# Tap stages with another order of evacuations and hooks, and gate chunks with one load beside the chunk at work

## The chip, the core and the metric

The kernel runs on one core of a Trainium2 chip. The metric is the device time of the program in microseconds (us); three runs of the kernel before gave a median of 1817.9 us (1817.29 to 1822.03). A profile is one further execution, which took 1812.46 us.

The engines are called as in the profile: PE is TensorE (PEld its weight loads), DVE is VectorE, ACT is ScalarE, POOL is GpSimd, SP is the engine that issues most transfers (DMAs). Each engine works through its own queue in order and waits on semaphores that others raise.

## What is computed

The input is x with shape (4, 256, 56, 56), all in float32. Four layers follow each other, each of the form x + f(gn(x)), where gn is a group norm over 32 groups of 8 channels.

```
layer 0, involution:  h = reduce_w . x;  kern = span_w . h + span_b   (7x7 taps for each of 16 groups and each pixel)
                      out[c, p] = sum over taps k of kern[group(c), k, p] * x[c, p + k]
layer 1:              two 3x3 convolutions with batch norms and relu, and a residual
layer 2, involution:  as layer 0, with a batch norm and relu after the reduction, a batch norm and relu at the end
layer 3, gates:       cf = mean over the image of real(fft2(xn)), per channel;  cf = sigmoid(cf @ W.T + b)
                      sf = real(fft2(mean over channels of xn)), per pixel
                      out = x + xn * cf + xn * sf,    xn = gn(x)
```

The mean of a two-dimensional Fourier transform is its input's first element, so cf needs only the pixel (0, 0) of every channel. sf is two small matrix products with cosines and sines of the 56x56 mean over the channels.

## The kernel before

`involution_layer` does layer 0 and, called a second time, layer 2; `conv_layer` lies between them and isn't touched. The loop of an involution runs over eight units, a unit being an image b (0 to 3) and a half cb of its channels (128 each). Each unit has two stages.

**Tap stage** (`tap_matrices`, L569). It makes the tap matrices kt of the unit in 32 steps, n = 0 to 31. In each step PE writes six matmuls (L580; the profile counts twelve[...]) into one PSUM tile of two banks. Then one engine moves the result with its bias to kt in SBUF: ACT in six instructions (L591) when n % 3 is 0, DVE in one (L598) otherwise. The pool `banks` has four such tiles, so PE can be at most four steps ahead of the evacuations. After step n the functions in `hooks[n]` are called: they put small pieces of other work at that place in each engine's queue. `place(hooks, g, (n1, n2, ...))` puts the generator g's successive pieces after steps n1, n2 and so on. A matmul of a hook takes a tile of the same pool.

**Column stage** (`apply`, L610). For each of seven columns tx, 8 pixels wide, PE multiplies the windows xw of the column with kt (L622), ACT and DVE gather the partial sums (`un`, L637 and L642), and in layer 2 DVE adds the result into the image block xs (L649). `next_windows` (L398) and `next_strip` (L362) prepare the column three further on: PE transposes a strip (L396), ACT copies it to xw (L408), and four transfers on SP's queue move it to the other row phases of xw (L414, L416). `late[tx]` holds functions that are called after column tx.

The hooks that the change touches lie in layer 2. Call (pb, pc) the unit before the one at work.

- `norm_of` (`norm_steps`, L200): six pieces, namely aggregate the statistics (DVE, L204), average over groups (PE, L207), copy and square the difference (DVE, L210 to L215), average again (PE, L218), add epsilon and take the power −1/2 (DVE L138, POOL L139), and make the shift (DVE, L222). It is placed at (2, 6, 7, 11, 12, 13) for the norm of layer 3. In the stages of units 1 and 2 of layer 2 a second norm is placed, that of layer 2's last image.
- `channel_mean` (L677) at (13, 17): small DVE work (L683, L694), then the mean over the channels on PE (L702, L705, two PSUM tiles), which is stored to DRAM.
- `gate_factors` (L720) when a whole image is done (pc is 1): loads the weights w3 (L725), multiplies them with the first pixels (PE, L732) and takes the sigmoid (ACT, L739), makes sf (PE, L748 and L762) and stores it to DRAM (L772).
- `load_step` (L963) loads the next image's block into the oldest of three blocks.

`gate_chunk` (L777) does layer 3's last line for images 0 to 2 on POOL, while the next image's units run. An image has 14 chunks: seven row bands j of 448 pixels times two halves cb. A chunk has two parts: the load of its piece of x from DRAM into one of three `gx` tiles, with the band's row of sf broadcast to all partitions (tile `sfb`, two buffers) when cb is 0; then four POOL operations (L789, L794, L795, L796) and the store (L797). `next_load` and `next_gate` start the next chunk's first and second part. POOL also issues these transfers. In the unit (b, 0) two loads stand after column 1 and a pair (gate, load) after each of columns 2 to 6; in (b, 1) three pairs stand in the tap stage (16, 22, 28) and six after columns 0 to 5. POOL's queue has little else in layer 2, so it works through the chunks as fast as transfers and the power of L139, which stands between them, let it.

At the end of a layer `in_order` ties every engine's instructions to the order in which the code wrote them. No scheduler moves them.

Of the kernel before, what the change touches and what calls it, by code (L numbers as in the profile page):

```python
# [10 lines left out]
F32 = mybir.dt.float32  # L11
AF = mybir.ActivationFunctionType
# [59 lines left out]
def net_kernel(  # L72
# [207 lines left out]
    def involution_layer(layer, xin, xout, red, span, sb, xs_of, ahead=None, pending=None):  # L280

        with ExitStack() as es:
# [23 lines left out]
            if layer == 0:  # L306
                load(0, 0, (2, 2, 2, 1))
                load(0, 1, (2, 2, 2, 1))

                nc.scalar.copy(norm_sb[:, 3, B - 1, 1, :], mhalf)  # L310

            red_sb = wpool.tile([P, NB, 2, R], F32, name="red_sb")

# [255 lines left out]
            def tap_matrices(b, cb, hooks):  # L569

                hp = h_of[b]
                kt = big.tile([Q, GB, TP // PB, NT, PB], F32, name="kt")
                for n in range(GB // 2 * TP // PB):
                    gp, pb = divmod(n, TP // PB)
                    ps = two_banks()
                    for k in range(PB):
                        py, px = divmod(pb * PB + k, TX)
                        z0 = ZF - py * QX - px
                        for i in range(2):
                            nc.tensor.matmul(  # L580
                                ps[:Q, i, k * NT : (k + 1) * NT],
                                z_sb[i * R : (i + 1) * R, cb * GB // 2 + gp, z0 : z0 + Q],
                                hp[i * R : (i + 1) * R, py, px].rearrange("p a t -> p (a t)"),
                                start=True,
                                stop=True,
                            )
                    g0, p0 = 2 * gp, pb * PB
                    if n % 3 == 0:
                        for i in range(2):
                            for k in range(PB):  # L590
                                nc.scalar.activation(  # L591
                                    kt[:, g0 + i, pb, :, k],
                                    ps[:Q, i, k * NT : (k + 1) * NT],
                                    AF.Identity,
                                    bias=zb_sb[:, cb * GB + g0 + i, p0 + k : p0 + k + 1],
                                )
                    else:
                        nc.vector.tensor_tensor(  # L598
                            kt[:, g0 : g0 + 2, pb],
                            ps[:Q, :, : PB * NT].rearrange("q i (k t) -> q i t k", k=PB),  # L600
                            zb_sb[:, cb * GB + g0 : cb * GB + g0 + 2, p0 : p0 + PB]
                            .unsqueeze(2)
                            .to_broadcast([Q, 2, NT, PB]),
                            ALU.add,
                        )
                    for h in hooks.get(n, ()):
                        h()
                return kt
# [68 lines left out]
            def channel_mean(b, cb):  # L677
# [39 lines left out]
                nc.sync.dma_start(m2_of[cb], m_dram[b][cb].rearrange("j (r w) -> (j r) w", w=W))  # L717
                yield

            def gate_factors(b):  # L720


                w3_sb = [dead(b, 1, 4 * CR * W + ci * C, C) for ci in range(NB)]
                for ci in range(NB):
                    nc.sync.dma_start(w3_sb[ci], w3[ci * P : (ci + 1) * P])  # L725
                cf = small.tile([P, NB], F32, name="cf")
# [36 lines left out]
                scale = small.tile([P, NB], F32, name="gscale")  # L763
                bias = small.tile([P, NB], F32, name="gbias")
                nc.vector.tensor_mul(scale, cf, norms[3][b][0])
                nc.vector.tensor_scalar_add(scale, scale, 1.0)
                nc.vector.tensor_mul(bias, cf, norms[3][b][1])
                gate_of[b] = scale, bias
                yield
                sf = small.tile([H, W], F32, name="sf", bufs=1)  # L770
                nc.vector.tensor_copy(sf, ps[:H, :W])
# [2 lines left out]

            sf_of, gate_of = {}, {}

            def gate_chunk(b, j, cb):  # L777

                rstd, shift = norms[3][b]
                at = slice(j * CR * W, (j + 1) * CR * W)  # L780
                if cb == 0:
                    sf_of[b] = work.tile([P, CR * W], F32, name="sfb", bufs=2)
                    nc.gpsimd.dma_start(sf_of[b], sf_dram[b][j : j + 1].to_broadcast([P, CR * W]))
                sf = sf_of[b]
# [4 lines left out]
                nc.gpsimd.tensor_scalar(  # L789
                    xn, xs, rstd[:, cb : cb + 1], shift[:, cb : cb + 1], ALU.mult, ALU.add  # L790
                )

                scale, bias = (t[:, cb : cb + 1] for t in gate_of[b])
                nc.gpsimd.tensor_scalar(xs, xs, scale, bias, ALU.mult, ALU.add)  # L794
                nc.gpsimd.tensor_tensor(xn, xn, sf, ALU.mult)  # L795
                nc.gpsimd.tensor_tensor(xs, xs, xn, ALU.add)  # L796
                nc.gpsimd.dma_start(ov[b, cb][:, at], xs)  # L797
                yield

# [193 lines left out]
            for u, (b, cb) in enumerate(units):  # L993
                hooks = hooks0 if u == 0 else {}
                if prev is not None:
# [726 lines left out]
```

## Time and profile before

| what | value |
|---|---|
| median of three runs | 1817.9 us |
| the profiled execution | 1812.46 us, its span 1810.7 us |
| mean granted clock of PE | 0.979 |
| PE busy | 1720.8 us, 95% of the span |
| DVE, ACT, POOL busy | 1375.4, 842.2, 430.0 us |
| layer 0's tap stages | 24.8 to 28.2 us each |
| layer 2, first tap stage to the last column stage's end | 1259.6 to 1778.4 us |
| of this, tap stages | 30.0, 31.8, 36.1, 29.1, 32.7, 28.7, 34.1, 31.0 us |
| of this, column stages | 28.3, 34.5, 31.5, 35.6, 34.4, 36.2, 32.3, 32.5 us |

How to read the profile: a row of a group or of a timeline has line, engine and operation, the tiles written and read, and in brackets how long the engine sat idle before it and what ended that. A stage is named here by the time at which it starts, counted from the start of the span. "Clock" is the share of its full clock that PE was granted; there are short periods at one half. A busy PE isn't necessarily at its peak. The chain of waits follows the work that ended last back from the end, at each step to what released it.

### The profile page before, as it was taken

How to read it: one execution, taken by the hardware profiler on the slowest of the kernel's cores; microseconds unless marked ns; L12 is line 12 of the kernel's file. 1: busy time of each engine (PE TensorE's matmuls, PEld its weight loads, DVE VectorE, ACT ScalarE, POOL GpSimd, SP SyncE). 2: the span in 40 equal slices, each digit the busy share in tenths (PEclk: the TensorE clock that was granted, in tenths of full speed). 3: DMA queues.
4: the chain of work that ended last, by engine and by line, in shares of the span. 5: the costliest groups of instructions: out<-in, count | busy, mean ns of one | idle time of the engine just before them, and what ended most of it. 6: DMA issues, size and time to landing. Idle time of an engine off the chain costs nothing.

```text
span 1810.7 us, 55835 instructions
## 1 busy us (share of the span) xinstructions
PE 1720.8 (95%) x24034; PEld 1514.9 (84%) x24034; DVE 1375.4 (76%) x2729; ACT 842.2 (47%) x1981; POOL 430.0 (24%) x626
## 2 busy tenths in 40 slices
PE   7999999999989999999999999997999999899988
PEld 6998989889878988998899889985988887887876
DVE  3787777776689988898889888875777677677775
ACT  3566556555532322322232222113767567577564
POOL 2333433245210000000000000000000374563572
PEclk9999999999989999999999999998999999999997
DMA  2545534454651201120121111031534566665653
GB/s 85 158 154 165 164 119 143 159 159 116 209 174 49 69 26 63 63 70 30 59 73 59 41 60 34 34 135 49 161 132 149 168 218 188 202 210 168 169 156 127
DMA packets 66004, 215.77 MB, mean 119 GB/s; under 512 B 13237, under 2 KB 20926, under 8 KB 62046
## 3 DMA queue, kind: packets, MB, share of 16 engines
q1 hardware_dynamic: 48718, 145.24, 25.7%
q0 software_dynamic: 14688, 64.78, 11.3%
q8 instruction: 190, 3.11, 0.7%
q10 hardware_dynamic: 2352, 2.18, 0.4%
q14 instruction: 56, 0.46, 0.1%
HBM read 76.30 MB, written 49.15 MB: 69 GB/s over the span
## 4 chain that ended last, share of the span: by engine, by line
PE 76%; DVE 9%; ACT 6%; DMA 4%; issue 2%; POOL 2%; SPq 1%; ACTq 0%; POOLq 0%; DVEq 0%
PE mm L1493 19%; PE ps L580 18%; PE ps L622 14%; PE mm L1411 10%; PE mm L1382 5%; PE ps L396 5%; DMA xw<-xw 4%; ACT kt L591 3%; PE ps L459 2%; DVE un L642 1%; DVE kt L598 1%; ACT xw L408 1%; ACT hp L478 1%; SPq L414 1%; DVE res L1486 1%
## 5 line engine op out<-in xcount | busy, mean ns | idle before, releaser
L580 PE MATMUL ps<-hp,z_sb 64*126 64x133 f32 x6144 | 392.1, 281 | 16.2 <-ACT kt L591 7.0
L622 PE MATMUL ps<-kt,xw 126*32 126x48 f32 (+1 forms) x12544 | 379.0, 236 | 24.1 <-DMA xw<-xw 12.1
L622 PEld LDWEIGHTS ps<-kt,xw 126*32 126x32 f32 (+1 forms) x12544 | 341.9, 122 | 68.2 <-issue 46.3
L580 PEld LDWEIGHTS ps<-hp,z_sb 64*126 64x126 f32 x6144 | 369.1, 187 | 34.6 <-ACT kt L591 12.7
L598 DVE TENSOR_TENSOR kt<-ps,zb_sb 126x798 f32<-126x798 f32 x336 | 319.8, 981 | 90.1 <-PE ps L580 89.5
L1493 PE MATMUL mm<-v,u_sb 128*128 128x280 f32 (+1 forms) x1728 | 385.0, 385 | 3.4 <-DVE v L1318 3.4
L1493 PEld LDWEIGHTS mm<-v,u_sb 128*128 128x128 f32 x1728 | 327.9, 190 | 57.5 <-DVE v L1318 3.8
L591 ACT ACTIVATE kt<-ps,zb_sb 126x133 f32<-126x133 f32 x1056 | 306.9, 442 | 96.2 <-PE ps L580 95.6
L1411 PE MATMUL mm<-v,u_sb 128*128 128x252 f32 (+1 forms) x936 | 212.3, 388 | 3.4 <-DVE v L1302 3.4
L1411 PEld LDWEIGHTS mm<-v,u_sb 128*128 128x128 f32 x936 | 178.3, 192 | 33.8 <-issue 3.5
L1530 POOL DMA_DIRECT2D x<-xs x24 | 13.1, 546 | 683.2 <-DVE xs L1529 427.4
L642 DVE SCALAR_TENSOR_TENSOR un<-ps,s,un 128x240 f32<-128x240 f32 x224 | 102.5, 457 | 85.7 <-ACT un L637 81.5
L642 DVE SCALAR_TENSOR_TENSOR un<-ps,par_sb,un 128x240 f32<-128x240 f32 x224 | 98.3, 457 | 87.1 <-ACT un L635 82.8
L1478 ACT ACTIVATE res<-xs,shift,norm_sb 128x1120 f32<-128x1120 f32 (+1 forms) x24 | 30.2, 1259 | 236.3 <-DVE xs L1529 107.3
L408 ACT COPY xw<-ps 126x896 f32<-126x896 f32 x112 | 101.4, 906 | 47.9 <-PE ps L396 37.7
L647 POOL TENSOR_TENSOR xs<-un,xs 128x240 f32<-128x240 f32 x112 | 72.3, 664 | 192.4 <-DVE un L642 192.3
L396 PE MATMUL ps<-ident_sb,strip_sb 128*126 128x128 f32 x784 | 111.7, 283 | 6.1 <-POOL strip_sb L381 5.8
L635 ACT ACTIVATE un<-ps,par_sb 128x240 f32<-128x240 f32 x112 | 50.1, 448 | 115.7 <-PE ps L622 113.4
L1382 PE MATMUL mm<-xs,u_sb 128*128 128x126 f32 (+1 forms) x792 | 98.6, 277 | 1.3 <-DVE xs L1345 0.9
L396 PEld LDWEIGHTS ps<-ident_sb,strip_sb 128*126 128x126 f32 x784 | 84.9, 142 | 17.0 <-POOL strip_sb L381 6.9
L637 ACT ACTIVATE un<-ps,bn_t,s 128x240 f32<-128x240 f32 x112 | 60.0, 538 | 83.3 <-PE ps L622 72.1
L1382 PEld LDWEIGHTS mm<-xs,u_sb 128*128 128x128 f32 x792 | 94.5, 191 | 2.4 <-issue 1.0
(254 smaller groups left out, 1925.8 us busy)
## 6 DMA issues: line engine op xcount, KB each, us to landing
xw<-xw SPq DMA_DIRECT2D x168, 252.0 KB
xw<-xw SPq DMA_DIRECT2D x224, 126.0 KB
xw<-xw POOLq DMA_DIRECT2D x56, 252.0 KB, 4.7
xs<-x SPq DMA_DIRECT2D x24, 560.0 KB
x<-xs POOLq DMA_DIRECT2D x8, 1568.0 KB, 8.2
xs<-x SPq DMA_DIRECT2D x8, 1568.0 KB
xs<-in_x_dram SPq DMA_DIRECT2D x6, 1568.0 KB
x<-xs SPq DMA_DIRECT2D x6, 1568.0 KB
```

The source lines that it names most:

```text
L396: nc.tensor.transpose(ps[:Q, k * P : (k + 1) * P], flat[:, k * Q : (k + 1) * Q], ident_sb)
L408: nc.scalar.copy(xw[:, :NSB, :], ps[:Q, : NSB * P].rearrange("q (n c) -> q n c", n=NSB))
L580: nc.tensor.matmul(ps[:Q, i, k * NT : (k + 1) * NT], z_sb[i * R : (i + 1) * R, cb * GB // 2 + gp, z0 : z0 + Q], hp[i * R : (i + 1) * R, py ...
L591: nc.scalar.activation(kt[:, g0 + i, pb, :, k], ps[:Q, i, k * NT : (k + 1) * NT], AF.Identity, bias=zb_sb[:, cb * GB + g0 + i, p0 + k : p0 ...
L598: nc.vector.tensor_tensor(kt[:, g0 : g0 + 2, pb], ps[:Q, :, : PB * NT].rearrange("q i (k t) -> q i t k", k=PB), zb_sb[:, cb * GB + g0 : cb ...
L622: nc.tensor.matmul(v[m * j : m * j + m, i, :, k * TP : (k + 1) * TP], xw[:, window(ty), m * j : m * j + m], kt[:, ng * j : ng * j + ng, :, ...
L637: nc.scalar.activation(part, o[0], AF.Identity, bias=bn["t4"][:, cb : cb + 1], scale=bn["s4"][ng][:, 0, cb : cb + 1])
L642: nc.vector.scalar_tensor_tensor(part, o[e], s, part, ALU.mult, ALU.add)
L647: nc.gpsimd.tensor_tensor(dst, u, dst, ALU.add)
L1382: nc.tensor.matmul(ps[:, co * m : (co + 1) * m], u[ci][:, co * P : (co + 1) * P], v2[:, e, : n // 2, ci * WT : (ci + 1) * WT], start=(ci = ...
L1411: nc.tensor.matmul(ps, u1_sb[:, ci, dy, k, co * P : (co + 1) * P], v[:, k, dy * NB + ci : (dy + n - 1) * NB + ci + 1 : NB, :], start=(j == 0),
L1493: nc.tensor.matmul(ps, u2_sb[:, ci, dy, k, co * P : (co + 1) * P], v[:, k, dy * NB + ci : (dy + n - 1) * NB + ci + 1 : NB, :], start=(j == 0),
```

## The change

Six things are changed, all in `involution_layer`.

- ACT's first instruction is a Sigmoid, in place of a copy. What it writes is overwritten later.
- ACT takes the steps with n % 3 equal to 2, not 0 (both involutions). So ACT has 10 steps in a stage and DVE 22, where it was 11 and 21.
- The second norm in units 1 and 2 of layer 2 moves to (15, 19, 20, 24, 25, 26).
- `gate_factors` begins at hook 8 with its load of w3, which goes into the two `sfb` buffers, and no longer into a dead part of the image block (the last image excepted).
- The gate is written as out = (sf + (cf + 1/rstd)) * xn − shift/rstd. It needs three POOL operations with one tensor operand and one with two, where it was two and two.
- The chunks: one load at hook 20 of the unit (b, 0), two bands of sf after column 0, then pairs (load, gate) after columns 1 to 5; four pairs in the tap stage of (b, 1) at 14, 18, 22, 26; five after its columns 0 to 4. The load of a chunk now stands in front of the chunk before it, so it writes the `gx` tile that was stored two chunks ago. The sf of band j + 2 is loaded at the end of band j.

```
-                nc.scalar.copy(norm_sb[:, 3, B - 1, 1, :], mhalf)
+                nc.scalar.activation(norm_sb[:, 3, B - 1, 1, :], mhalf, AF.Sigmoid)
...
-                    if n % 3 == 0:
+                    if n % 3 == 2:
...
+            def new_sf():
+                return work.tile([P, CR * W], F32, name="sfb", bufs=2)
...
-                w3_sb = [dead(b, 1, 4 * CR * W + ci * C, C) for ci in range(NB)]
+                w3_sb = [new_sf()[:, :C] if b < B - 1 else dead(b, 1, 4 * CR * W + ci * C, C) for ci in range(NB)]
...
-                nc.vector.tensor_mul(scale, cf, norms[3][b][0])
-                nc.vector.tensor_scalar_add(scale, scale, 1.0)
-                nc.vector.tensor_mul(bias, cf, norms[3][b][1])
-                gate_of[b] = scale, bias
+                nc.vector.reciprocal(back, rstd)
+                nc.vector.tensor_add(cfx, cf, back)
+                nc.vector.scalar_tensor_tensor(back, shift, -1.0, back, ALU.mult, ALU.mult)
+                gate_of[b] = cfx, back
...
+            def load_sf(b, j):
+                sf_of[b, j] = new_sf()
+                nc.gpsimd.dma_start(sf_of[b, j], sf_dram[b][j : j + 1].to_broadcast([P, CR * W]))
...
-                if cb == 0:
-                    sf_of[b] = work.tile([P, CR * W], F32, name="sfb", bufs=2)
-                    nc.gpsimd.dma_start(sf_of[b], sf_dram[b][j : j + 1].to_broadcast([P, CR * W]))
...
-                nc.gpsimd.tensor_scalar(xs, xs, scale, bias, ALU.mult, ALU.add)
-                nc.gpsimd.tensor_tensor(xn, xn, sf, ALU.mult)
-                nc.gpsimd.tensor_tensor(xs, xs, xn, ALU.add)
+                nc.gpsimd.tensor_scalar(xs, sf_of[b, j], 1.0, cfx, ALU.mult, ALU.add)
+                nc.gpsimd.tensor_tensor(xs, xs, xn, ALU.mult)
+                nc.gpsimd.tensor_scalar(xs, xs, 1.0, back, ALU.mult, ALU.add)
+                if cb == 1 and j + 2 < NCHUNK:
+                    load_sf(b, j + 2)
...
-                        place(hooks, g, (19, 20, 22, 23, 25, 26))
+                        place(hooks, g, (15, 19, 20, 24, 25, 26))
...
-                            place(hooks, gate_factors(pb), (17, 24, 27, 28, 30, 31))
+                            place(hooks, gate_factors(pb), (8, 24, 27, 28, 30, 31))
+                            chunks.extend(gate_chunk(pb, j, c) for j in range(NCHUNK) for c in range(NB))
+                            for n in (20,):
+                                hooks.setdefault(n, []).append(next_load)
...
-                        for n in (16, 22, 28):
-                            hooks.setdefault(n, []).extend((next_gate, next_load))
+                        for n in (14, 18, 22, 26):
+                            hooks.setdefault(n, []).extend((next_load, next_gate))
...
-                        chunks.extend(gate_chunk(b - 1, j, c) for j in range(NCHUNK) for c in range(NB))
-                        late[1] += [next_load, next_load]
-                    for tx in range(2, NTX) if cb == 0 else range(NTX - 1):
-                        late[tx] += [next_gate, next_load]
+                        late[0] += [lambda b=b, j=j: load_sf(b - 1, j) for j in range(2)]
+                    for tx in range(1, 6) if cb == 0 else range(NTX - 2):
+                        late[tx] += [next_load, next_gate]
```

More of the change, by code (lines that the diff above doesn't have):

```diff
@@ L762, in gate_factors @@
                 nc.tensor.matmul(ps[:H, :W], half, cs2_sb, start=True, stop=True)
-                scale = small.tile([P, NB], F32, name="gscale")
-                bias = small.tile([P, NB], F32, name="gbias")
-                nc.vector.tensor_mul(scale, cf, norms[3][b][0])
-                nc.vector.tensor_scalar_add(scale, scale, 1.0)
-                nc.vector.tensor_mul(bias, cf, norms[3][b][1])
-                gate_of[b] = scale, bias
+                cfx = small.tile([P, NB], F32, name="gscale")
+                back = small.tile([P, NB], F32, name="gbias")
+                rstd, shift = norms[3][b]
+                nc.vector.reciprocal(back, rstd)
+                nc.vector.tensor_add(cfx, cf, back)
+                nc.vector.scalar_tensor_tensor(back, shift, -1.0, back, ALU.mult, ALU.mult)
+                gate_of[b] = cfx, back
                 yield
@@ L780, in gate_chunk @@
                 at = slice(j * CR * W, (j + 1) * CR * W)
-                if cb == 0:
-                    sf_of[b] = work.tile([P, CR * W], F32, name="sfb", bufs=2)
-                    nc.gpsimd.dma_start(sf_of[b], sf_dram[b][j : j + 1].to_broadcast([P, CR * W]))
-                sf = sf_of[b]
                 xs = gx_tile()
@@ L791, in gate_chunk @@
                 )
[L793 to L796, printed above, removed]
+                cfx, back = (t[:, cb : cb + 1] for t in gate_of[b])
+                nc.gpsimd.tensor_scalar(xs, sf_of[b, j], 1.0, cfx, ALU.mult, ALU.add)
[3 more added lines that the diff above has]
+                    load_sf(b, j + 2)
                 nc.gpsimd.dma_start(ov[b, cb][:, at], xs)
```

## The prediction

> **What bounds the kernel now.** I read the page first, then a table of windows, one row for each tap and column stage, then the chain of waits inside layer 2, then the engines' timelines around each wait found there. The page names the bound:
>
> ```profile
> PE 1720.8 (95%) x24034; PEld 1514.9 (84%) x24034; DVE 1375.4 (76%) x2729; ACT 842.2 (47%) x1981; POOL 430.0 (24%) x626
> ```
>
> TensorE is the only full engine, so a stage can only gain what TensorE waits in it. The windows show where (after the length: busy us and instructions of PE, PEld, DVE, ACT, POOL, then clock, DMA share, GB/s):
>
> ```profile
> 159.30:184.10 24.80, 24.64 (x396) 23.87 (x395) 21.92 (x32) 19.83 (x67) 3.88 (x6) 1.00 0.46 163
> 1384.20:1420.30 36.10, 32.11 (x441) 28.35 (x440) 25.23 (x50) 23.50 (x73) 1.10 (x2) 0.95 0.36 127
> 1451.80:1480.90 29.10, 26.80 (x419) 24.28 (x418) 23.88 (x36) 21.58 (x70) 23.00 (x30) 1.00 0.72 240
> 1516.50:1549.20 32.70, 30.39 (x436) 26.46 (x435) 25.69 (x44) 22.45 (x72) 4.10 (x5) 1.00 0.43 153
> 1549.20:1583.60 34.40, 30.63 (x827) 27.52 (x826) 21.20 (x48) 18.18 (x26) 24.86 (x32) 0.90 0.74 205
> ```
>
> A layer-0 tap stage (first row) takes 24.8 us with almost no wait: 32 steps of about 0.75 us. Layer 2's last seven take 31.8, 36.1, 29.1, 32.7, 28.7, 34.1 and 31.0 us. Their hooks add at most 4.4 us of matmuls (channel mean 2.0, gate factors 1.8, second norm 0.6); the rest is wait or a lowered clock. Column stages without gates take 28.3 us (1289.6) or 34.5 (with the bottleneck); with gates 31.5 to 36.2. The chain inside layer 2 names what is waited for (start us, us, what):
>
> ```profile
> 1406.56 0.99 DVE kt L598
> 1409.63 1.75 ACT kt L591 x6
> ...
> 1539.02 2.30 DMA xs<-in_w_dram
> ...
> 1561.10 8.11 DMA xw<-xw
> ```
>
> And the engines' timelines give the single waits:
>
> ```profile
> 1404.57 0.30 PEld L207 LDWEIGHTS ps<-mv,gavg_sb 128*128 128x128 f32 x2 [1.11 <-ACT kt L591]
> 1408.31 0.30 PEld L218 LDWEIGHTS ps<-d,gavg_sb 128*128 128x128 f32 x2 [1.31 <-ACT kt L591]
> 1411.42 1.39 PEld L580 LDWEIGHTS ps<-hp,z_sb 64*126 64x126 f32 x12 [0.95 <-ACT kt L591]
> 1468.15 0.16 PEld L702 LDWEIGHTS ps<-one,mean 128*32 128x32 f32 x8 [1.25 <-DVE kt L598]
> 1411.39 1.28 ACT L739 ACT_TABLE_LOAD   x1
> 1465.63 1.57 DVE L694 TENSOR_SCALAR mean<-cmean,norm_sb 128x32 f32<-128x32 f32 x2
> 1517.46 1.07 DVE L649 SCALAR_TENSOR_TENSOR xs<-un,xs 128x240 f32<-128x240 f32 x1
> ```
>
> GpSimd is at 24% but not harmless: its groups in layer 2 (mean ns after the busy time) are
>
> ```profile
> L795 POOL TENSOR_TENSOR gn<-gn,sfb 128x448 f32<-128x448 f32 x42 | 49.0, 1166 | 0.0
> L796 POOL TENSOR_TENSOR gx<-gx,gn 128x448 f32<-128x448 f32 x42 | 48.7, 1160 | 3.3
> L794 POOL TENSOR_SCALAR gx<-gx,gscale,gbias 128x448 f32<-128x448 f32 x42 | 31.7, 756 | 4.2
> L789 POOL TENSOR_SCALAR gn<-gx,norm_sb 128x448 f32<-128x448 f32 x42 | 31.7, 754 | 24.4 <-DMA gx<-x 18.1 <-DVE un L642 5.3
> ```
>
> In DVE's timeline L649 takes 0.41 us when no GpSimd arithmetic runs, 0.86 on average (13 cases) under a GpSimd tensor_tensor; L694 takes 0.23 alone and 0.89 under one.
>
> [...] in the new program one table load is left. [...] a gx load lands 4.0 us after issue at 1551.8, and 8.6 us after at 1566.9, among xw transfers.
>
> **The change part by part.** Each sum is TensorE wait.
>
> *Sigmoid at the start, and w3 loaded at hook 8.* The first Sigmoid costs about 0.26 us (L739's rows) for a copy of 0.19, while ACT then idles 2.58 us for a DMA: nothing. The table load at 1411.39 goes. At hook 24 of the stage at 1384.2, step 25 waited 0.95 for ACT's step 24 (now VectorE's, done sooner) and step 26 0.19 for the Sigmoid: −1.1. At 1516.5 the w3 matmuls waited for their transfer, issued 1538.6 (0.69 + 0.49 of idle weight loads: −1.1), at 1648.6 2.0 us (the answer names ACT, which ended just then; w3's last packets run to 1672.5): −2.0. Now w3 is issued right behind the store of xs, some 16 us earlier, and its buffers' last gate is long over. **−4.2.** On SP nothing waits behind it; the next block's load, which waited for w3's readers (issued 1542.2 in the stage at 1516.5), can go at about 1538.5, and at both times lands before the column stage's xw transfers.
>
> *Second norm of layer 2's units 1 and 2 (stages 1318.0, 1384.2).* The statistics were aggregated at hook 19 and multiplied at hook 20, then used at 22 and multiplied at 23. One step (0.75 us) isn't enough: L204 ends at 1404.45 and L207 starts at 1404.57; the square ends 1408.2 and L218 starts 1408.31. Waits of 1.11 + 1.31 in each of two stages. The new places 15→19 and 20→24 leave four steps. Two tiles out of four PSUM buffers still cost about 0.2 each: **−4.0.**
>
> *ACT takes steps 2, 5, ... 29 (10 of them) instead of 0, 3, ... 30 (11).* In 16 stages one step moves from 6 × 0.29 us on ACT to 0.98 on VectorE. Three places count. (a) Hook 17: before, the channel mean's big tile took over step 15's buffer, an ACT step of 1.75 us, and its first matmuls queued behind VectorE's step 14. Now 15 is VectorE's, and 14 ACT's, so VectorE has 0.98 us more between the hook-13 work and step 15. Waits there: 0.32 in four stages, and 1.25, about 1.0 and 1.1 in the three (1451.8, 1583.6, 1714.9) where a gate chunk ran under L694. The new chunk issues a load (0.54) first and begins with two tensor_scalars, so L694 meets no tensor_tensor. Of 4.6 us: **−3.5**. (b) Start: VectorE now does 0, 1, [L1078], [L204], 3, 4 in a row, 0.98 + 0.95 + 0.54 + 0.33 + 0.95 + 0.9 = 4.65 us from 1386.09, so step 7 starts 0.4 us later than now; but ACT's strip no longer holds step 4 (wait 0.83), and L218 at hook 11, behind a wait for ACT of 0.25, comes at the same 9.8 us into the stage: 0, in layer 0 as well. (c) End: steps 30 and 31 are both VectorE's. At 182.63 it starts the first and ends the second at 184.55, where ACT ended step 30 at 184.38. Columns begin at 184.1 and need both: **+2.7** in 16 stages. The second norm in layer 0's stages (96.5, 213.2, 332.5) falls on worse places: step lengths now 1.09 + 0.92 + 1.09, 0.85 over; I work out 1.0: **+0.5.** The three new small operations at hook 30 have rows at 0.14 to 0.16 us in the last gates, like those that they replace.
>
> *Chunks: one load beside the chunk at work, three tensor_scalars and one tensor_tensor.* Arithmetic goes from 0.75 + 0.76 + 1.17 + 1.16 to 3 × 0.75 + 1.16, −0.43 us; with issues (0.54, 0.59, half of 0.55) and the 0.6 of gaps 5.6 becomes 5.2. The wait for a buffer's store (6.4 us in all) goes. GpSimd is off the path; what shows is when it runs. With 5 + 4 + 5 chunks for 5 + 3 + 6 the last should end before the next tap stage. Today it runs 3.4 us into it and slows L649 (1.07 and 0.85 us at 1517 to 1520): −1.0 there, −1.0 at 1714.9. **−2.0**; less tensor_tensor under the columns, **−0.5.**
>
> *DMA in the column stages.* The xw waits (1.1 at 1433, 3.8 at 1565, 2.1 at 1695) come at columns 3 to 5. Bytes are the same, and one of three first loads moves to hook 20. But two sfb loads go out at once, and the first store comes about 2 us sooner. Between 1558 and 1569, 2.3 MB moved in 11 us (208 GB/s): two transfers (0.46 MB) more in front of the xw cost 2.2 us, two fewer gain as much. I take **+1.0** over all.
>
> Sum: −4.2 − 4.0 − 3.5 + 2.7 + 0.5 − 2.0 − 0.5 + 1.0 = −10.0 us. The profiled execution took 1812.46 us (span 1810.7): 1802.5 for it. The timed runs' median is 1817.9, 5.4 us above; the same −10 gives 1808.
>
> **Rivals.** *The xw transfers lose (slower).* Place: columns 3 to 5 of six column stages with gates. For: DMA share is already 0.74, and above 0.9 at the wait. Price 2.2 us per two more transfers ahead, three give 3.3 × 6 = 20: 1808 + 20 = 1828. It decides from 2.6 us per stage on, where it beats the gain by 5.5. Against: the loads depend on one buffer each, so GpSimd slows itself when transfers are late. *The phase costs more (no change).* If VectorE's crowded start, of which I cost nothing, loses 0.4 us (step 7's delay) in all 16 stages, 6.4, and hook 17 gains half, the sum is −10 + 6.4 + 1.8 = −2: 1816. For: VectorE has 22 steps × 0.95 = 21 us of a 24.8 us stage. Against: its work catches up by hook 11. *The xw waits go (faster).* 7.0 at the three places above and about 2.5 at 1758 to 1768 in the last stage; with the +1.0 not spent, that is −20: 1798. For: one load fewer at the start, and the block's load earlier. Against: xw alone fills half of the DMA time.
>
> **How the numbers follow.** Forecast 0.50, xw waits go 0.16, no change 0.20, slower 0.14. A measurement tells 0.3% (5.5 us) from no change. The first two are faster: 0.66; same 0.20; slower 0.14. The range leaves out half of the two outer cases: 1800 to 1821; the likeliest case's own is 1802 to 1812, from half to one and a half of the sum.
>
> **What will show it.** Right: no table load at L739; no wait at L735 and L207/L218 above 0.3 us; the tap stages that now take 36.1, 32.7 and 34.1 come 2 to 4 us shorter; GpSimd idle at each tap stage's start in units after gates. Wrong if column stages with gates grow by over 2 us each, or layer 0's tap stages (24.8 and 26.2) by over 0.5. A throttle that falls on other stages (clock 0.90 at 1549.2 here) would move single stages without meaning.

## The result, and the profile after

| | before | after |
|---|---|---|
| median of five timed runs | 1820.47 us | 1800.78 us |
| their spread | 1817.29 to 1826.22 | 1798.91 to 1807.65 |
| the profiled execution, its span | 1812.46, 1810.7 us | 1803.55, 1801.8 us |

The ratio is 0.9907, with a 95% interval of 0.9882 to 0.9931: about 17 us less (12.6 to 21.5). A second measurement of the same kernel, told below, gave 0.9897 (0.9865 to 0.993). The forecast was 10 us less, so the sign is right and the size too small. The two profiled executions differ by only 8.9 us, and the experiments show why two single executions can't settle the size.

The page of the kernel after has one line for the engines:

```profile
PE 1717.5 (95%) x24034; PEld 1511.1 (84%) x24034; DVE 1389.1 (77%) x2745; ACT 815.6 (45%) x1884; POOL 403.8 (22%) x626
```

TensorE has the same 24034 matmuls and still sets the pace. ACT is busy 27 us less and VectorE 14 us more, GpSimd 26 us less. The table of windows for the same five stages as in the prediction (layer 0's stage, three tap stages, the column stage after the third; after the length, busy us and instructions of PE, PEld, DVE, ACT and POOL, then clock, DMA share and GB/s):

```profile
159.30:184.10 24.80, 24.65 (x417) 23.88 (x408) 22.62 (x34) 18.21 (x61) 3.89 (x6) 1.00 0.47 166
1384.90:1416.00 31.10, 30.07 (x441) 26.68 (x440) 25.89 (x51) 20.80 (x66) 1.65 (x3) 1.00 0.46 156
1451.60:1478.70 27.10, 26.66 (x419) 24.39 (x419) 23.70 (x37) 20.55 (x64) 14.10 (x21) 1.00 0.60 200
1513.90:1544.00 30.10, 29.32 (x437) 26.01 (x436) 24.97 (x44) 20.69 (x66) 2.15 (x4) 1.00 0.49 168
1544.00:1578.80 34.80, 29.44 (x829) 25.83 (x828) 20.54 (x48) 18.17 (x26) 22.91 (x33) 1.00 0.74 197
```

The tap stages of 36.1, 29.1 and 32.7 us became 31.1, 27.1 and 30.1. TensorE's idle time in them fell from 4.0, 2.3 and 2.3 us to 1.0, 0.4 and 0.8, and the clock of the first rose from 0.95 to 1.00. The column stage did not gain (34.4 to 34.8): its clock rose from 0.90 to 1.00, but TensorE idled 5.4 us in it where it had idled 3.8. In the timelines of the kernel after, the places of the second norm (L207, L218) and of the gates' weights w3 (now L735), and the one table load that is left (at the start, L310, where the kernel before has one too), read:

```profile
1403.05 0.30 PEld L207 LDWEIGHTS ps<-mv,gavg_sb 128*128 128x128 f32 x2
1407.05 0.30 PEld L218 LDWEIGHTS ps<-d,gavg_sb 128*128 128x128 f32 x2
1408.22 0.52 PEld L735 LDWEIGHTS ps<-first,sfb 128*128 128x128 f32 x4 [0.42 <-ACT kt L591]
1535.60 0.97 PEld L735 LDWEIGHTS ps<-first,sfb 128*128 128x128 f32 x8
```
```profile
L310 ACT ACT_TABLE_LOAD x1 | 1.3, 1283 | 2.9 <-issue 2.9
```

The brackets of 1.11 and 1.31 us at L207 and L218 are gone, and w3 is waited for in no stage. One wait of 0.42 us for an ACT step stays at L735. GpSimd's groups in layer 2 now have one tensor_tensor in place of two:

```profile
L799 POOL TENSOR_TENSOR gx<-gx,gn 128x448 f32<-128x448 f32 x42 | 48.4, 1153 | 3.5
L793 POOL TENSOR_SCALAR gn<-gx,norm_sb 128x448 f32<-128x448 f32 x42 | 31.3, 745 | 10.7 <-DMA gx<-x 9.4
L800 POOL TENSOR_SCALAR gx<-gx,gbias 128x448 f32<-128x448 f32 x42 | 27.6, 658 | 4.3
L798 POOL TENSOR_SCALAR gx<-sfb,gscale 128x448 f32<-128x448 f32 x42 | 27.5, 655 | 10.3 <-DMA sfb<-sf 6.5
```

The two tensor_scalars with one constant factor take 0.66 us, not the 0.75 that the prediction used, so a chunk's arithmetic fell by 0.6 us and not 0.43.

### The profile page after: what moved, and what is told of

Same layout as the page of the kernel before. It is cut to its first block, busy times and chain, and to the rows that moved or that the text cites. A ratio compares the mean times of both kernels' runs of the same rounds, so it can differ in the third digit from the quotient of the medians.

```text
span 1801.8 us, 55766 instructions
## 1 busy us (share of the span) xinstructions
PE 1717.5 (95%) x24034; PEld 1511.1 (84%) x24034; DVE 1389.1 (77%) x2745; ACT 815.6 (45%) x1884; POOL 403.8 (22%) x626
## 3 DMA queue, kind: packets, MB, share of 16 engines
q1 hardware_dynamic: 48718, 145.24, 25.9%
## 4 chain that ended last, share of the span: by engine, by line
PE 72%; DVE 16%; ACT 4%; DMA 3%; issue 3%; POOL 2%; SPq 1%; ACTq 0%; POOLq 0%; DVEq 0%
PE mm L1501 19%; PE ps L580 14%; PE ps L622 13%; PE mm L1419 10%; DVE kt L598 5%; PE mm L1390 5%; PE ps L396 3%; DVE un L642 3%; DMA xw<-xw 3%; PE ps L459 2%; DVE st L1086 1%; ACT kt L591 1%; ACT hp L478 1%; DVE res L1494 1%; PE ps L705 1%
## 5 line engine op out<-in xcount | busy, mean ns | idle before, releaser
L622 PE MATMUL ps<-kt,xw 126*32 126x48 f32 (+1 forms) x12544 | 380.1, 235 | 31.4 <-issue 18.0
L622 PEld LDWEIGHTS ps<-kt,xw 126*32 126x32 f32 (+1 forms) x12544 | 340.9, 121 | 77.5 <-issue 50.2
L580 PE MATMUL ps<-hp,z_sb 64*126 64x133 f32 x6144 | 383.5, 279 | 12.3 <-DVE kt L598 4.7
L580 PEld LDWEIGHTS ps<-hp,z_sb 64*126 64x126 f32 x6144 | 363.6, 185 | 28.3 <-DVE kt L598 6.4
L598 DVE TENSOR_TENSOR kt<-ps,zb_sb 126x798 f32<-126x798 f32 x352 | 333.1, 980 | 59.5 <-PE ps L580 59.1
L591 ACT ACTIVATE kt<-ps,zb_sb 126x133 f32<-126x133 f32 x960 | 280.1, 442 | 107.9 <-PE ps L580 107.8
L1419 PEld LDWEIGHTS mm<-v,u_sb 128*128 128x128 f32 x936 | 177.5, 191 | 31.8 <-issue 1.4
L1538 POOL DMA_DIRECT2D x<-xs x24 | 13.1, 546 | 682.3 <-DVE xs L1537 427.5
L396 PEld LDWEIGHTS ps<-ident_sb,strip_sb 128*126 128x126 f32 x784 | 84.6, 141 | 18.6 <-POOL strip_sb L381 6.6
L139 POOL TENSOR_TENSOR norm_sb<-norm_sb,mhalf 128x1 f32<-128x1 f32 x32 | 19.7, 619 | 350.1 <-DVE norm_sb L138 350.0
```

The source lines that it names most:

```text
L396: nc.tensor.transpose(ps[:Q, k * P : (k + 1) * P], flat[:, k * Q : (k + 1) * Q], ident_sb)
L580: nc.tensor.matmul(ps[:Q, i, k * NT : (k + 1) * NT], z_sb[i * R : (i + 1) * R, cb * GB // 2 + gp, z0 : z0 + Q], hp[i * R : (i + 1) * R, py ...
L591: nc.scalar.activation(kt[:, g0 + i, pb, :, k], ps[:Q, i, k * NT : (k + 1) * NT], AF.Identity, bias=zb_sb[:, cb * GB + g0 + i, p0 + k : p0 ...
L598: nc.vector.tensor_tensor(kt[:, g0 : g0 + 2, pb], ps[:Q, :, : PB * NT].rearrange("q i (k t) -> q i t k", k=PB), zb_sb[:, cb * GB + g0 : cb ...
L622: nc.tensor.matmul(v[m * j : m * j + m, i, :, k * TP : (k + 1) * TP], xw[:, window(ty), m * j : m * j + m], kt[:, ng * j : ng * j + ng, :, ...
L1419: nc.tensor.matmul(ps, u1_sb[:, ci, dy, k, co * P : (co + 1) * P], v[:, k, dy * NB + ci : (dy + n - 1) * NB + ci + 1 : NB, :], start=(j == 0),
```

## The experiments

Microseconds are the ratio times the median of before on that chip, with the interval in brackets. Three chips were used: one for the kernel before again, ACT's steps, the hooks and the first run of the chunks; a second for the gate's form, the places, the one-row stores and the later chunks; a third for the second norm, the kernel without the chunks, and the repeats of the chunks and of the kernel after. In code, line numbers move by up to 8 with each edit.

### The kernel before, measured against itself

No edit.

> The kernel before once more, for how much one execution differs from another. Theory A (each stage repeats itself, but for the throttle): layer 2's tap stages add up to 253.5 us again within 3 us, and the seven column stages before the last to 232.8 within 3 us plus half of what half-clock periods fall on them; the ratio of times is 1.000. Theory B (the waits for xw differ from execution to execution): the column stages with gates differ by 5 us or more in the sum, and the profile's 1810.7 us span was a lucky one; the next is 1815 or more.

Measured: 0.9998, −0.4 us [−4.4, +3.5]. The instructive part is its profile: the span was 1820.7 us against 1810.7 of the first, and layer 2's column stages took 275.8 us against 265.4, while its tap stages took 250.9 against 253.4. Column stages of one and the same kernel differ by 10 us from one execution to the next. So the 7.3 us by which they seem longer in the first profile of the kernel after (272.7) are no effect of the change. The tap stages repeat within about 3 us in all, so traces are compared there.

### ACT's steps alone

```
-                    if n % 3 == 0:
+                    if n % 3 == 2:
```

> Only the choice of ACT's steps (n % 3 equal to 2). By the forecast: hook 17 -3.5 (0.3 in four stages, 0.6 to 1.0 in the three under a gate chunk), stage ends +2.7, layer 0's second norm +0.5: together -0.3 us, ratio 1.000; the wait of step 3 or 4 at the stages' start goes and comes back at step 6. Rival (VectorE's crowded start costs 0.4 us per stage): +6, ratio 1.003.

Measured: 0.9996, −0.7 us [−4.4, +2.9]. The rival by which VectorE's crowded start would cost some 6 us is out. But the −3.5 us which the prediction booked at hook 17 aren't this edit's alone. In the timelines of this kernel, stage at 1459.5 (weight loads, then VectorE):

```profile
1474.50 0.19 PEld L702 LDWEIGHTS ps<-one,mean 128*32 128x32 f32 x8 [1.06 <-issue]
1475.33 0.16 PEld L705 LDWEIGHTS ps<-xs,mean 128*32 128x32 f32 x8 [0.64 <-DVE kt L598]
```
```profile
1472.68 1.71 DVE L694 TENSOR_SCALAR mean<-cmean,norm_sb 128x32 f32<-128x32 f32 x2
```

L694's pair still takes 1.71 us, and the channel mean is waited for twice, 1.06 and 0.64 us, where the kernel before had one wait of 1.25. In the four stages without a chunk at this place the matmuls' wait at L705 (0.24 us each) is gone, as forecast; in the three with one the wait is longer. What delays hook 17 in those is the GpSimd chunk, not ACT's step 15.

### The hooks alone, and the second norm alone

The Sigmoid at the start, w3 in the sf buffers at hook 8, and the second norm's places:

```
-                        place(hooks, g, (19, 20, 22, 23, 25, 26))
+                        place(hooks, g, (15, 19, 20, 24, 25, 26))
...
-                            place(hooks, gate_factors(pb), (17, 24, 27, 28, 30, 31))
+                            place(hooks, gate_factors(pb), (8, 24, 27, 28, 30, 31))
```

> Only the Sigmoid at the start, w3 at hook 8 in the sfb buffers, and the second norm's new places; ACT's steps and the chunks as before. By the forecast -4.2 - 4.0 = -8.2 us, ratio 0.9955, the stages that take 36.1, 32.7, 34.1 and 31.8 us shorter by 3.1, 1.1, 2.0 and 2.0. Rival (the gain in the tap stages is the phase's and the chunks'): -4 us or less.

Then only the first of the two pairs of lines:

> Of the hooks, only the second norm of layer 2's units 1 and 2 is moved; the table load, the w3 load and the gates' hooks stay as before. Forecast in the prediction: -4.0 us (waits of 1.11 and 1.31 us in each of two stages, less 0.2 for each tile). The traces' step lengths gave -5.2. So ratio 0.997 to 0.998. If instead the hooks' gain lies almost all in the gates' waits, -1 us or less (0.9995).

Measured: the hooks 0.9942, −10.5 us [−14.0, −7.1]; the second norm alone 0.9975, −4.5 us [−7.1, −2.2]. The forecasts were −8.2 and −4.0. The difference of the two, 6.0 us for the gates' hooks (from two chips), was forecast as 4.2; the intervals don't separate these. The stage that has the second norm and no gates took 31.8 us before and 29.5 in both kernels.

### The chunks alone, twice

The gate's form, its loads and its places as in the kernel after; ACT's steps, the Sigmoid, w3 and the second norm as before.

> Only the gate's new form and the new places of loads, sf loads and chunks; w3, second norm and ACT's steps as before. By the forecast -2.0 - 0.5 + 1.0 = -1.5 us, ratio 0.999. Rival, from comparing the two traces (columns with gates lost 4.1, 3.7 after allowing for the throttle, and 3.3 us at 1416, 1544 and 1673 us): tap stages' starts gain 4, columns lose 10: +6 us, ratio 1.003. It would show in the column stages of the units (1,0), (2,0) and (3,0) taking 34 to 36 us, and TensorE waiting there for xw transfers by 4 us or more each.

> The chunks alone a second time, because the gate's new form alone gave -1.5 us and the new places alone -0.7, which is not the -9.3 of both together. If both are needed together (only a shorter chunk at the earlier places is done before the next tap stage), the ratio is again 0.994 to 0.996 (-7 to -11 us). If the first measurement was chance, 0.998 to 1.000 (-0 to -4 us).

Measured: 0.9949, −9.3 us [−12.4, −6.4], and on another occasion 0.9964, −6.5 us [−9.3, −3.8]. The forecast was −1.5, so this term was too small.

### The gate's form alone, and the places alone

```
-                nc.gpsimd.tensor_scalar(xs, xs, scale, bias, ALU.mult, ALU.add)
-                nc.gpsimd.tensor_tensor(xn, xn, sf, ALU.mult)
-                nc.gpsimd.tensor_tensor(xs, xs, xn, ALU.add)
+                nc.gpsimd.tensor_scalar(xs, sf, 1.0, cfx, ALU.mult, ALU.add)
+                nc.gpsimd.tensor_tensor(xs, xs, xn, ALU.mult)
+                nc.gpsimd.tensor_scalar(xs, xs, 1.0, back, ALU.mult, ALU.add)
```

> The kernel before with the gate's new form alone (one GpSimd tensor_tensor and three tensor_scalars per chunk for two and two); loads, places, w3, second norm and ACT's steps as before. Theory P [...]: the chunk change gains because VectorE's L649 and L694 meet half as much tensor_tensor; 42 chunks lose 1.16 us of it each; then this run has most of the 9.3 us of the chunk change: -6 us or more, ratio 0.9965 or less. Theory S (the schedule): the gain is from chunks that end before the next tap stage and from the loads' order; then -2 us or less here, ratio 0.999.

and the other half, the new order of loads and the new places with the old two tensor_tensors:

> The kernel before with the chunks' new places, loads and sf loads, in the gate's old form. Theory P: -3 us or less, ratio 0.998 or more. Theory S: -6 us or more, ratio 0.9965 or less, and the tap stages of the units (2,0), (3,0) start without a wait above 0.8 us.

Measured: 0.9992, −1.5 us [−3.5, +0.4], and 0.9996, −0.7 us [−3.1, +1.6]. Neither half gives what both give together, so neither of the two theories holds by itself. (These two runs and the two of the chunks come from different chips, each compared with the kernel before on its own.) One reason is visible at hook 17, in the first tap stage that has chunks. For the form alone: the tensor_tensor on GpSimd, L694 on VectorE, and the weight load that waits for it:

```profile
1468.86 1.15 POOL L796 TENSOR_TENSOR gx<-gx,gn 128x448 f32<-128x448 f32 x1
1469.01 1.18 DVE L694 TENSOR_SCALAR mean<-cmean,norm_sb 128x32 f32<-128x32 f32 x2
1471.14 0.16 PEld L702 LDWEIGHTS ps<-one,mean 128*32 128x32 f32 x8 [1.19 <-DVE kt L598]
```

For the places alone:

```profile
1472.52 0.58 POOL L789 DMA_DIRECT2D gx<-x  x1
1474.64 1.14 POOL L798 TENSOR_TENSOR gn<-gn,sfb 128x448 f32<-128x448 f32 x1
1474.10 1.71 DVE L694 TENSOR_SCALAR mean<-cmean,norm_sb 128x32 f32<-128x32 f32 x2
1476.77 0.16 PEld L702 LDWEIGHTS ps<-one,mean 128*32 128x32 f32 x8 [1.59 <-DVE kt L598]
```

For both (the chunks alone):

```profile
1470.10 1.14 POOL L799 TENSOR_TENSOR gx<-gx,gn 128x448 f32<-128x448 f32 x1
1469.52 0.67 DVE L694 TENSOR_SCALAR mean<-cmean,norm_sb 128x32 f32<-128x32 f32 x2
1471.13 0.16 PEld L702 LDWEIGHTS ps<-one,mean 128*32 128x32 f32 x8 [0.57 <-DVE kt L598]
```

GpSimd stands at the power of the norm (L139) and starts its chunk when that is done, so its tensor_tensor comes at the moment of L694. With both edits it starts 0.58 us after L694's start, and L694 is through in 0.67: the load has gone ahead of the chunk, and the tensor_tensor comes after the whole tensor_scalar whose result it now reads. In the other two kernels L694 is caught: with the form alone the tensor_tensor is already running; with the places alone it starts 0.54 us after L694's start and L694 lasts to its end. The margin is some hundredths of a microsecond, yet all three stages of each kernel show it: L139 waits for VectorE's L138, and L694 follows L138 on VectorE behind one evacuation, so the two queues meet in step. Over these three stages and the four without a chunk, TensorE's waits at L702 and L705 sum to 3.9 us with the form alone, 5.1 with the places alone and 2.0 to 2.1 with both, where before had 3.5 to 3.8. So some 3 us of what only both edits give lie here. In the kernel after, with ACT's new steps, VectorE reaches L694 1.4 us after L138 and not 2.4 us, well ahead of the tensor_tensor:

```profile
1466.02 1.15 POOL L799 TENSOR_TENSOR gx<-gx,gn 128x448 f32<-128x448 f32 x1
1464.42 0.82 DVE L694 TENSOR_SCALAR mean<-cmean,norm_sb 128x32 f32<-128x32 f32 x2
1465.70 0.16 PEld L702 LDWEIGHTS ps<-one,mean 128*32 128x32 f32 x8
1466.17 0.16 PEld L705 LDWEIGHTS ps<-xs,mean 128*32 128x32 f32 x8 [0.32 <-DVE kt L598]
```

L694 is done 0.78 us before the tensor_tensor starts, and one wait of 0.32 us is left. The pair still takes 0.82 us, where it takes 0.46 with no GpSimd arithmetic beside it: it is longer beside a tensor_scalar too, though less than beside a tensor_tensor.

### The kernel after without the chunks, and the kernel after again

The first has ACT's steps and the hooks as after, and everything of the chunks as before.

> The kernel after with the chunks left as before (the gate's form, its loads and its places), so ACT's steps, the Sigmoid, w3 and the second norm alone. If the chunks are worth 9 us beside the rest as they were alone, this is -8 to -11 us against before (ratio 0.994 to 0.9955) and 8 to 10 us slower than the kernel after on this chip. If the chunks are worth what was forecast (1.5 us net) and their single measurement came out large by chance, this is -16 us or more (0.991), the same as the kernel after.

> The kernel after as it is, on the chip on which the other three of this set run. If the change's gain is as large as its parts measured one by one (phase 0.7, hooks 10.5, chunks 9.3, together 20.5 us), the ratio to the kernel before is 0.989 (0.987 to 0.991, about -20 us). If the first measurement's middle was right, 0.991 (-17 us). If the parts that were measured singly gain the same microseconds twice, -13 us or less (0.993).

Measured: without the chunks 0.9963, −6.7 us [−9.8, −3.6]; the kernel after 0.9897, −18.7 us [−24.5, −12.7]. So beside the rest of the change the chunks are worth about 12 us on this chip (the two medians, 1811.16 and 1798.05, differ by 13.1, and the slowest of six runs with the new chunks is faster than the fastest of 22 with the old). Alone they gave 6.5 there. The alternative, that their single measurement came out large by chance, falls.

This kernel also shows that ACT's new steps and the old chunks do not fit at hook 17: its three tap stages with chunks take 30.9, 29.8 and 29.0 us (28.6, 28.8 and 29.4 with the hooks alone), with 1.5 us waited at L702 and L705 in each, as in ACT's steps alone. With the new chunks they take 27.1, 27.9 and 27.8.

### Where a full DMA would show

In the kernel after, each chunk stores one partition only, so that 127 of 128 rows of the gates' output for images 0 to 2 (9.6 MB) are left out:

```
-                nc.gpsimd.dma_start(ov[b, cb][:, at], xs)
+                nc.gpsimd.dma_start(ov[b, cb][:1, at], xs[:1])
```

> The changed kernel, but each chunk of the gates stores one partition of its result and not all 128, so this leaves out 42 x 0.23 MB = 9.6 MB of writes; all arithmetic and all loads stay. Theory D (in columns with gates the xw transfers wait because the 16 DMA engines are full): TensorE's waits for xw fall by half or more, the four column stages after a whole image (35.6, 34.8, 33.9, 33.1 us in the changed kernel's profile) come near 30 us, together -12 us against the changed kernel, ratio to the kernel before about 0.984. Rival (xw waits come from SP's own issue, 3.2 us per column, and the chain transpose, copy, transfer): no change against the changed kernel, ratio 0.991.

And in the kernel after, GpSimd first waits for column 2's statistics in the units (b, 0), with the pairs after columns 3 to 6 and not 1 to 5, and six pairs in place of five in (b, 1):

```
-                        late[0] += [lambda b=b, j=j: load_sf(b - 1, j) for j in range(2)]
-                    for tx in range(1, 6) if cb == 0 else range(NTX - 2):
+                        late[3].append(lambda: nc.gpsimd.tensor_copy(small.tile([P, 1], F32, name="gm"), st[:, 2, 0:1]))
+                        late[3] += [lambda b=b, j=j: load_sf(b - 1, j) for j in range(2)]
+                    for tx in range(3, NTX) if cb == 0 else range(NTX - 1):
```

> The changed kernel, but in the units (b, 0) GpSimd waits for the statistics of column 2 before it loads sf and begins the chunks: pairs after columns 3 to 6, four in the tap stage, six in the columns of (b, 1). Theory D: columns 3 to 5 no longer share the DMA engines with chunks, the windows for the next unit that do have a tap stage of slack: -8 us against the changed kernel, ratio 0.987. Rival: the chunks only move, the waits move with them to columns 4 to 6 of (b, 0) and to (b, 1), and the last chunk runs into the next tap stage: 0 to +4 us, ratio 0.991 to 0.993.

Measured: 0.9878, −22.2 us [−26.7, −17.6], and 0.9898, −18.6 us [−21.5, −15.5], both against before. Leaving out nearly all of the gates' stores gains about 4 us over the kernel after (measured on another chip), within the intervals, and TensorE's waits in the columns hardly move. Starting the chunks later moves the waits for xw to column 6 (2.8 to 3.2 us in each of the three units) and gains nothing. So neither of the forecast gains of 12 and 8 us came: the gates' stores and the chunks' start are no lever of more than a few microseconds here.

### All traces side by side

Worked out from the trace of each profiled execution, for layer 2 from its second tap stage on: the length of the seven tap stages; TensorE's waits of over 0.15 us in them and in the seven column stages; and half of the time at half clock. All in us.

| kernel | tap stages | waits in them | waits in columns | half-clock loss |
|---|---|---|---|---|
| before, twice | 223.4, 221.6 | 18.9, 18.4 | 17.1, 24.7 | 8.5, 10.2 |
| ACT's steps | 217.5 | 16.3 | 20.0 | 6.8 |
| form | 220.3 | 17.4 | 20.0 | 10.2 |
| places | 222.8 | 18.8 | 17.4 | 6.8 |
| second norm | 217.3 | 14.1 | 25.9 | 8.5 |
| hooks | 211.7 | 10.3 | 21.2 | 5.1 |
| chunks, twice | 217.3, 217.6 | 15.2, 15.1 | 19.0, 21.3 | 8.5, 5.1 |
| without chunks | 209.5 | 9.8 | 20.7 | 3.4 |
| after, twice | 202.7, 204.2 | 4.5, 4.7 | 23.5, 16.3 | 1.7, 0.0 |
| one-row stores | 203.8 | 4.1 | 22.5 | 3.4 |
| later chunks | 204.7 | 5.6 | 17.8 | 8.5 |

The tap stages lost 19 us from before to after. About 14 are waits; the rest is mostly time at half clock in these stages (3.4 and 4.6 us before, none after). The columns' waits scatter between 16 and 26 us, with no order by kernel.

The waits in the tap stages divide by place: those at the channel mean of hook 17 (L702, L705), and of the others those in a stage's first 10 us and those later, which lie mostly at the second norm and the gates' hooks. In us:

| kernel | first 10 us | hook 17 | later |
|---|---|---|---|
| before, twice | 5.7, 4.7 | 3.8, 3.5 | 9.5, 10.1 |
| ACT's steps | 4.5 | 4.4 | 7.5 |
| form | 4.1 | 3.9 | 9.4 |
| places | 4.3 | 5.1 | 9.4 |
| chunks, twice | 4.1, 3.9 | 2.1, 2.0 | 9.1, 9.2 |
| hooks | 4.7 | 3.6 | 1.9 |
| without chunks | 4.4 | 4.4 | 1.0 |
| after, twice | 3.1, 3.7 | 0.8, 0.7 | 0.6, 0.3 |

## Why the prediction was right or wrong

**The likeliest case** held: faster, through waits of TensorE in layer 2's tap stages, with columns and layer 0 paying little. Its size did not: −10 forecast, −17 and −18.7 measured. The measured 1800.78 lies outside the likeliest case's own range of 1802 to 1812 and just inside the whole range; −18.7 from the same 1817.9 would lie just outside.

The waits themselves were forecast well. By the last table they fell by some 14 us in the tap stages: 1.8 at the stages' starts, 2.9 at hook 17 and 9.3 at the second norm and the gates. The terms for these were −2.0, −3.5 and −8.2, together −13.7. What the forecast lacked is what came on top of the waits: the tap stages became 19 us shorter, not 14, and some 4 of the other 5 us are half clock, a term that was put at nothing. Against that stood +3.7 for ends, layer 0 and columns (with −0.5 among the columns), of which the traces show a part.

The rival in which the waits for xw go gave 1798, close to the time measured, but by luck and not by its mechanism: the columns' waits did not fall measurably. In the stage at 1544.0 after, the chain of waits still has

```profile
1551.62 8.79 DMA xw<-xw
...
1567.08 1.59 issue
```

where before had 8.11 us for that transfer.

**Second norm, −4.0.** Measured −4.5 [−7.1, −2.2] alone, and the waits at the second norm's L207 and L218 are gone. Right.

**Sigmoid and w3, −4.2.** Together with the norm −10.5 where −8.2 was forecast; the waits at the gates' own weight products (L732, now L735) fell from 2.8 us to 0.3 between the first traces of before and after, and the 0.95 us behind step 24 is gone. That the table load of 1.28 us at L739 would go was an assumption of the prediction; the traces show one load left of two, 1.28 us at L310. Right in mechanism and, within the interval, in size. The prediction's sign of being right, no wait above 0.3 us at L735 and at L207 and L218, failed by little: 0.42 us at L735, and 0.32 us at L207 before layer 3's norm, in five stages, as in ACT's steps alone.

**ACT's steps, −0.3 in all.** Measured −0.7 [−4.4, +2.9]; right as a sum, within that interval, but wrong in one step. Hook 17 was booked at −3.5 under this edit. The kernel after has nearly that (2.9 us), but the edit alone makes hook 17 worse by 0.7 us, the chunks alone better by 1.6: the gain needs both, and of the chunks both halves. The argument that L694 meets no tensor_tensor was right; that it then runs free was not: with a tensor_scalar beside it the pair took 0.82 us, not 0.46 (why, no trace shows). Without the −3.5 the edit's other terms would have given +3, so the sum's agreement is in part luck; where this kernel's tap stages gain the 5 us that its one trace shows (222.5 to 217.5) is not settled, and the timed runs do not show them. The stage's end (+2.7 in 16 stages, 0.17 each) shows in layer 0, where the first column takes 3.63 us for 3.49, 0.14 more. The tap stages of layer 0 sum to 206.7 us for 206.1; +0.5 was forecast.

**Chunks, −2.0, −0.5 and +1.0.** This term was too small: −9.3 and −6.5 alone, some −12 beside the rest. Part of that is hook 17, booked elsewhere (above). With the chunks alone the tap stages become 5 us shorter (222.5 to 217.5), and 3.5 of it are waits: 1.2 at the stages' starts, 1.6 at hook 17, 0.7 later. What remains of the measured gain, 1.5 to 4 us, can't be placed, since columns vary more than that. The step that the last chunk ends before the next tap stage is right in direction: before, its arithmetic ran up to 7.9 us into it, after no more than 0.4, or 1.8 in the second profile. The +1.0 for the columns is neither shown nor excluded: the columns' waits average 21.4 us in the seven executions with the old places and 19.5 in the five with exactly the new ones, but without the gaps described in the last section they average 11.2 and 12.7. The parts listed for a chunk's length sum to 5.8 us, not 5.6; nothing rests on it.

**The throttle.** The prediction said that a throttle on other stages "would move single stages without meaning". The windows of before around its half-clock period in the stage at 1384.2 show what goes ahead of it:

```profile
1408.02:1411.44 3.42, 2.23 (x24) 2.04 (x24) 1.06 (x2) 1.79 (x7) 0.00 (x0) 1.00 0.02 5
1411.44:1414.86 3.42, 3.42 (x28) 3.23 (x30) 1.17 (x3) 1.65 (x3) 0.55 (x1) 0.50 0.99 326
```

A window in which TensorE idled 1.2 us (the second norm's L218 and the step behind it) is followed by one at half clock, in which 3.42 us of work do what 1.71 would. This period stands in that stage in all seven executions whose second norm is at the old places, between 1410 and 1415 us. In the six executions with hooks and norm moved together it is there once, at 1405.6, and with the norm moved alone it remains at 1409.8, where the gates still wait.

The 2.2 us called busy in the first window include matmuls that write a single column, such as

```profile
1409.51 1.05 PE L732 MATMUL ps<-first,xs 128*128 128x1 f32 x8
```

All changes of clock in the 14 traces' layer 2 fall on a grid of 3.413 us (in the first trace of before its half-clock periods last 3.41, 6.83, 3.41 and 3.41 us). Cut on that grid, and with matmuls of one column counted as idle, layer 2 has 2032 windows at full clock. All 36 with at least 1.9 us of idle are followed by half clock, none of the 1968 with less than 1.6, and 7 of the 28 between. So in these traces the limit lies between 1.6 and 1.9 us, about half of a window; no run was made to test it. If only the plain idle time is counted, all 28 windows with 1.8 us or more are followed by half clock, none under 0.6, and just 15 of the 301 between: the window above has 1.2 us of plain idle time and 2.4 with its one-column matmuls. That these count as idle is a reading of these two counts, not shown otherwise. The grid also fits a gap of 2.2 us at 1441.3 in the kernel after that no half clock followed: a boundary at 1442.36 divides it, and the two windows have 1.1 and 1.2 us of idle.

The idle time need not be one wait: before the period at 1698.16 in the trace of before, TensorE waited 0.42 and 1.73 us for xw in one window (2.1 us idle). So a wait that is removed takes with it, at times, 1.7 us more, half of a window at half clock. In the tap stages this loss fell from 3.4 and 4.6 us to none, about half of what the forecast missed. In the columns it comes and goes with the execution: the later chunks lost 8.5 us there and were as fast as the kernel after. No run isolates it.

**Not settled.** How the extra gain divides between half clock and columns. And whether ACT's steps help the kernel after at all: with the old chunks they look like a loss in the timed runs (−10.5 for the hooks alone, −6.7 with them, from two chips and with overlapping intervals) but not in the tap stages of the traces (211.7 and 209.5 us), and with the new ones L694 is clear of the tensor_tensor by a larger margin. The kernel after with n % 3 == 0 wasn't tried.

## What to carry to other kernels

Before a small operation is blamed on its own engine, look at what GpSimd does in the same half microsecond: two edits that did nothing clear of noise singly gave 6 to 9 us together, and some 3 of these came from moving a tensor_tensor by hundredths of a microsecond off one small VectorE operation. Price a wait of TensorE with the clock that follows it, not only with its length: here half clock followed once TensorE idled about half of a 3.41 us window (1.9 us or more in all 36 such windows), matmuls of one column counted as idle. And compare a kernel with itself once before reading two profiles: here the column stages of one kernel differed by 10 us, more than half of what the change was worth.

## What the hardware showed unexpectedly

In column stages TensorE sometimes stands still for 0.7 to 4 us with nothing to wait for ("issue"). In the second execution of before, with the DMA view of the same 5 us behind it:

```profile
1456.77 1.01 PE L622 MATMUL ps<-kt,xw 126*32 126x48 f32 x36 [3.91 <-issue]
```
```profile
q8 instruction: 1, 0.02, 1.6%
```

That single packet of 16384 bytes on the queue that the profile calls instruction ran from 1454.17 to 1455.41, and TensorE went on 1.4 us after it. There are 82 gaps of this kind over 0.6 us in layer 2 of the 14 traces. All stand before L622, and all end 1.2 to 1.8 us after a packet of 16384 bytes of this queue has landed, though the queue lands only 79 packets in layer 2's some 510 us of each trace, one in about 6.5 us. That TensorE waited for its own instructions is a guess from these times; no run tested it. The gaps over 0.6 us sum to 3.3 and 14.9 us in two executions of before and to 12.2 and 4.0 in two of after. These differences, 11.6 and 8.2 us, are about those of the spans (10.0 and 9.2 us).
